# A two-layer graph kernel on one core: layer 0's sum as seven half-block products instead of sixty-four tile products

## The chip, the cores and the metric

The kernel runs on one core of a Trainium2 chip. The metric is the device time of one execution in microseconds (us); before the change it is 1270.91 us, the median of three runs (1270.83 to 1271.21). The core has a matrix engine (TensorE, PE in the profile; PEld is its weight load), two engines for elementwise work on which much depends here (VectorE, DVE; ScalarE, ACT), GpSimd (POOL) and a queue engine (SyncE, SP) that issues most transfers. Each engine takes its instructions in order and waits for the others by semaphores.

## What is computed

There are 16 batches; each has 1024 nodes with 256 features (`x`) and an integer adjacency matrix `adj` (1024 x 1024, symmetric, ones on the diagonal, otherwise 0 or 1). Two layers follow one another, each with a residual sum and a normalization of the row:

```
# layer 0
e     = leaky(einsum('bid,bjd->bij', h * a[:, 0], h))     # a = a0 where adj == 1
alpha = sigmoid(where(adj == 1, e, -big))
x     = layernorm(x + einsum('bij,bjd->bid', alpha, h) + bias)
# layer 1
Hh    = einsum('bni,io->bno', x, W)
s, d  = Hh . a_src, Hh . a_dst
e     = where(adj != 0, exp(-leaky_relu(s[:, :, None] + d[:, None, :])), 0)
x     = layernorm(x + elu(einsum('bnm,bmo->bno', e, Hh) / rowsum(e)))
```

All products are in f32. A second path in the file covers adjacency values of 2 to 4 and doesn't run for these inputs.

## The kernel before, in words

Rows of 128 nodes are tiles: NT = 8 tiles a batch, HT = 4 tiles in a half; the features are ND = 2 pieces of 128. The order of the instructions is written out by hand, with no scheduler. Batch `b` runs layer 0 beside layer 1 of the batch before (`prev`) and the last normalization of the one before that (`done`). One turn of the loop over `b` has three stages on PE.

- **Strips.** `strip(b, jt)` makes row tile `jt` of the logits, from its diagonal to the right (L233: transposed x against x scaled by a0). ACT makes two tanh of it (L241, L242), VectorE takes their maximum (L243), and `finish` adds one, multiplies by the adjacency and writes `al` (L249). That is twice the sigmoid; the part below the diagonal is the mirror image of the part above it: `dump` transposes it in 32 x 32 squares on VectorE (L265) and sends it to DRAM in four transfers (L269), `gather` reads it back into `al` (L273), one strip later in the SP queue, and `mask` multiplies it by its adjacency (L280). Between the strips stand the eight `project` of layer 1 for `prev` (L411), and `share_p`, which sends a row of 1024 numbers to all partitions through DRAM (L431, L433).
- **Layer 0's sum.** `sum0` for each of the eight row tiles: `multiply0` is eight products of 128 x 128 by 128 x 256 into one accumulator (L348), `end0` halves it, adds the bias on VectorE (L358) and takes mean and variance (L301, L303). Two identities on the diagonal of `al`, added by GpSimd (L259), bring in the residual x. GpSimd takes the roots of the variances (L310 to L327), ACT scales the rows (`scale0`, L331). The rows go to DRAM (`save_x1`, L376) and come back in blocks of 32 (`fetch_x1`, L120), which VectorE turns (`turn_x1`, L387) into the transposed form that `project` needs. `weights` (L460, eight a batch, on VectorE) makes layer 1's matrix `e` meanwhile, `check_adj` runs on ACT.
- **Layer 1's sum.** For each of the eight row tiles eight products of 128 x 128 by 128 x 257 (L465). `elu` inverts the row sum on VectorE (L488, L489) and evicts the tile twice on ACT (L497, L498); `add` finishes the row and its statistics on VectorE (L503, L505, L301, L303).

`x` has two buffers (`load_x`, L94), so the next batch's x is loaded while this one is summed. `al`, `xT`, `xa`, `x1T` have one each. PSUM: three banks for strips (`ps_e`), two for `ps_t`, three for accumulators (`ps_acc`).

Of the kernel before, what the change touches and what calls it, by code (L numbers as in the profile page):

```python
# [18 lines left out]
P = 128  # L19
# [11 lines left out]
def one_kind_pass(  # L31
# [57 lines left out]
    def load_x(b, queues):  # L89
        xs[b] = two.tile([P, NT, D], F32, tag="x", name=f"x_{b}")  # L90
        rows = x[b].rearrange("(t p) d -> p t d", p=P)
        n = NT // len(queues)
        for g, queue in enumerate(queues):
            queue.dma_start(xs[b][:, ts(g, n), :], rows[:, ts(g, n), :])  # L94
# [43 lines left out]
    arow = two.tile([P, D], F32, tag="h", name="arow")[0:ND, 0:P]  # L138
    nc.scalar.dma_start(arow, a0.rearrange("(c p) o -> c (p o)", p=P))
# [16 lines left out]
    nc.vector.memset(ones, 1.0)  # L156

    warm = const.tile([P, 1], F32, tag="warm", name="warm")
# [4 lines left out]
    load_x(1, [nc.gpsimd])  # L163
# [4 lines left out]
    pcol = ps_e.tile([P, HALF], F32, tag="e", name="pcol")[:, 0:ND]  # L168
    nc.tensor.transpose(pcol, arow, ident[0:ND, 0:ND])
    nc.scalar.copy(acol, pcol)  # L170
# [11 lines left out]


# [9 lines left out]
    def turn_x(b, c):  # L193

        if c == 0:
            xas[b] = one.tile([P, ND, N], F32, tag="xa", name=f"xa_{b}")
        nc.vector.transpose(xTs[b][:, c, :], xTs[b][:, c, :])
        nc.scalar.mul(xas[b][:, c, :], xTs[b][:, c, :], acol[:, c : c + 1])
# [46 lines left out]
    def finish(b, jt, c0=0, c1=N):  # L245


        c0 = max(c0, jt * P)
        nc.vector.scalar_tensor_tensor(  # L249
            als[b][:, jt, c0:c1],  # L250
            tbs[b, jt][:, c0 - jt * P : c1 - jt * P],
            1.0,
            adjs[b, jt // HT][:, jt % HT, c0:c1],
            ALU.add,
            ALU.mult,
        )
        if c0 == jt * P:
            diag = als[b][:, jt, ts(jt, P)]
            nc.gpsimd.tensor_tensor(diag, ident2, diag, ALU.add)  # L259
# [17 lines left out]
    def mask(b, t):  # L277
        for js, rows in adj_rows(b, t + 1, NT, ts(t, P)):
# [27 lines left out]
    def rstd(mv, what):  # L306
# [3 lines left out]
        nc.gpsimd.tensor_scalar(ve, mv[:, :, 1], EPS, None, ALU.add)  # L310
# [10 lines left out]
    def center(mv, what):  # L321

        r = rstd(mv, what)
# [3 lines left out]
        nc.gpsimd.tensor_scalar(mr, mr, -1.0, None, ALU.mult)  # L327
        return [(r[:, t : t + 1], mr[:, t : t + 1]) for t in range(n)]
# [4 lines left out]
    x1s, mv0s, r0s = {}, {}, {}  # L333
# [3 lines left out]
    def sum0(b, t):  # L337
        multiply0(b, t)
        end0(b, t)

    def multiply0(b, t):
        if t == 0:
            x1s[b] = two.tile([P, NT, D], F32, tag="x1", name=f"x1_{b}")
            mv0s[b] = small.tile([P, NT, 2], F32, tag="mv0", name=f"mv0_{b}")
            r0s[b] = []
# [10 lines left out]
    def end0(b, t):  # L356
        y = x1s[b][:, t, :]
        nc.vector.scalar_tensor_tensor(y, accs[t], 0.5, bias_bc, ALU.mult, ALU.add)  # L358
        stats(y, mv0s[b][:, t, :], f"0_{b}_{t}")
        if t % HT == HT - 1:  # L360
            g = t // HT
            r0s[b] += center(mv0s[b][:, ts(g, HT), :], f"0_{b}_{g}")
# [3 lines left out]


    x1Ts, Hs, pqs, p_bcs, es = {}, {}, {}, {}, {}

    x1_rows = {}  # L370
# [26 lines left out]
    def project(b, t):  # L397
# [11 lines left out]
        pt = ps_acc.tile([P, D + 2], F32, tag="acc", name=f"pH_{b}_{t}")  # L409
# [9 lines left out]
        nc.scalar.activation(w, pt[:, 1:2], AF.Exp, scale=-SLOPE)  # L419
        nc.scalar.activation(pqs[b][:, :, t], pt[:, 0:2], AF.Exp, scale=SLOPE - 1.0)  # L420
        nc.scalar.mul(Hs[b][t][:, 0:D], pt[:, 2:], w)
# [51 lines left out]
    def elu(b, t, acc):  # L473

        if t == 0:
# [8 lines left out]
            mv1s[b] = small.tile([P, NT, 2], F32, tag="mv1", name=f"mv1_{b}")  # L484


        rinv = small.tile([P, 1], F32, tag="rinv", name=f"rinv_{b}_{t}")
        nc.vector.tensor_scalar(rinv, acc[:, D : D + 1], TINY, None, ALU.max)  # L488
        nc.vector.reciprocal(rinv, rinv)  # L489
# [40 lines left out]
    nc.sync.dma_start(bias_bc, bias.partition_broadcast(P))  # L530

# [12 lines left out]
    for t in range(NT):  # L544
# [12 lines left out]
        if t < 2:  # L557
            make_Wx(t)
        if t == 1:
# [4 lines left out]
        if t in (4, 5):  # L564
            scale0(0, 2 * t - 8)
            scale0(0, 2 * t - 7)
            turn_x(1, t - 4)
        if t == 5:
            save_x1(0, 0)
            fetch_x1(0, 0)  # L570

    for b in range(1, B):
# [3 lines left out]
        projects = [[0, 1], [2], [3], [4, 5], [6], [7], [], []]  # L576
        if prev == 0:

            projects = [[], [], [0, 1], [2, 3], [4, 5], [6, 7], [], []]
        for jt in range(NT):  # L580
            if jt == 4:
                mask(b, 0)
            strip(b, jt)
            if prev == 0 and jt < 2:
                scale0(0, HT + 2 * jt)
                scale0(0, HT + 2 * jt + 1)
            finish(b, jt)
# [4 lines left out]
            if prev == 0 and jt == 2:  # L592
                transpose_x1(0)
            if jt >= 1:
                gather(b, jt - 1)
            for t in projects[jt]:
                project(prev, t)
            if jt == 6:
                share_p(prev)
            if jt >= 6:  # L600
                mask(b, jt - 5)
        check_pq(prev)
        if not last:
            load_x(b + 1, [nc.sync])
# [3 lines left out]
        for t in range(NT):  # L608
            if 1 <= t < 5:
                mask(b, t + 2)  # L610
            for m in ([], [], [0, 1], [2], [3], [4], [5], [6, 7])[t]:
                weights(prev, m)
            if done >= 0:
                scale1(done, t)
                if t in (3, 7):
                    store(done, t - 3, HT)
            sum0(b, t)
            if t == 5 and not last:
                load_adj(b + 1, 0)
            if t in (5, 6):  # L620
                scale0(b, 2 * t - 10)
                scale0(b, 2 * t - 9)
            if t == 6:
                save_x1(b, 0)
            if t >= NT - CHECKS:
                check_adj(b, t - NT + CHECKS)
        if not last:
            load_adj(b + 1, 1)


        for t in range(NT):
            acc = acc1(prev, t, ps_acc, "acc")
            for m in range(NT):
                sum1(prev, t, acc, m)
            if last and t == 6:
                turn_x1(b, 1)
            if last and t == 3:
                turn_x1(b, 0)
            if last and t == 7:
                for m in range(2):  # L640
                    weights(b, m, 0, HT)
            elu(prev, t, acc)
            if last and t == 7:
                for m in range(2, 6):
                    weights(b, m, 0, HT)
            if t >= 1:
                add(prev, t - 1)
            if t == 0:
                fetch_x1(b, 0)
            if t in (1, 2):  # L650
                scale0(b, 2 * t + 2)
                scale0(b, 2 * t + 3)
            if t == 2:
                save_x1(b, 1)
            if t == 4:
                fetch_x1(b, 1)
                if not last:
                    turn_x1(b, 0)
            if not last and t in (3, 5):
                turn_x(b + 1, (t - 3) // 2)  # L660
            if not last and t == 6:
                turn_x1(b, 1)
            if last and t in (4, 6):
                t0 = (t - 4) // 2 * HT
                for n in range(HT):
                    project(b, t0 + n)
                share_half(b, t0)
        if not last:
            add(prev, NT - 1)
            r1s[prev] = center(mv1s[prev], f"1_{prev}")  # L670
# [520 lines left out]
```

## Time and profile before

| what | value |
|---|---|
| median of three runs | 1270.91 us |
| span of the profiled execution | 1268.6 us |
| one turn of the loop over b (600.37 to 678.40 us) | 78.03 us |
| of it: strips and projections | 22.56 us |
| of it: layer 0's sum | 27.63 us |
| of it: layer 1's sum | 27.84 us |
| VectorE busy in the turn | 58.20 us |
| ScalarE busy in the turn | 40.56 us |
| GpSimd busy in the turn | 17.89 us |

The loop makes fifteen such turns, from about 54 us to 1225 us; batch 0's layer 0 stands before them and batch 15's layer 1 behind them. An f32 product of 128 x 128 by 128 x n appears as two records in the profile, so the 64 products of a sum are 128 records.

### The profile page before, as it was taken

What the parts mean: (1) busy time and instruction counts of PE and PEld (TensorE: products, weight loads), DVE (VectorE), ACT (ScalarE), POOL (GpSimd) and SP (SyncE); (2) the same over time, 40 slices, a digit from 0 to 9 for tenths busy, and PEclk for the clock granted to TensorE, in tenths of its full rate; (3) what the DMA queues carried; (4) which work ended last, traced back from release to release, by engine and by line L of the source; (5) the groups of instructions that cost most, each with busy time, mean ns of one, the idle gap of its engine ahead of it and who ended that gap; (6) DMA issues with size and microseconds to landing.
All of it is one profiled execution on the core that took longest, in us unless ns stands there. A gap on an engine that the chain in (4) does not pass through costs nothing.

```text
span 1268.6 us, 17528 instructions
## 1 busy us (share of the span) xinstructions
PE 1259.2 (99%) x5476; PEld 1024.5 (81%) x5476; DVE 925.2 (73%) x2027; ACT 650.2 (51%) x1467; POOL 299.7 (24%) x605
## 2 busy tenths in 40 slices
PE   9999999999999999999999999999999999999997
PEld 7788787887878878788787887878778787887886
DVE  5686867868678686876868868687686877858657
ACT  4645645456353564545645445454455644456434
POOL 2212231212312122121222212223122231212213
PEclk9999999999999999999999999999999999999999
DMA  9489595795959869497694966949579595895422
GB/s 213 80 171 155 92 197 92 168 185 106 190 90 177 168 124 198 78 174 159 131 203 83 184 131 139 210 80 190 113 167 185 97 192 95 171 183 99 109 51 69
DMA packets 603832, 180.77 MB, mean 142 GB/s; under 512 B 482010, under 2 KB 585940, under 8 KB 603732
## 3 DMA queue, kind: packets, MB, share of 16 engines
q1 hardware_dynamic: 581760, 135.85, 54.4%
q0 software_dynamic: 21280, 43.06, 18.7%
q8 instruction: 46, 0.75, 0.3%
q10 hardware_dynamic: 692, 0.66, 0.1%
q14 instruction: 54, 0.44, 0.1%
HBM read 152.44 MB, written 60.62 MB: 168 GB/s over the span
## 4 chain that ended last, share of the span: by engine, by line
PE 98%; DVE 1%; ACT 0%; issue 0%; ACTq 0%; DVEq 0%
PE acc L348 35%; PE acc L465 34%; PE pe L233 20%; PE pH L411 9%; PE busy L146 0%; PE pal L288 0%; PE pxT L209 0%; DVE st L301 0%; DVE y L505 0%; DVE y L503 0%; PE prow L427 0%; ACT y L331 0%; ACT y_kept L331 0%; ACT L680 0%; DVE mv L303 0%
## 5 line engine op out<-in xcount | busy, mean ns | idle before, releaser
L348 PE MATMUL acc<-x,al 128*128 128x256 f32 x2048 | 445.5, 379 | 0.0
L465 PE MATMUL acc<-H,e 128*128 128x257 f32 x2032 | 444.9, 379 | 0.0
L465 PEld LDWEIGHTS acc<-H,e 128*128 128x128 f32 x2032 | 384.9, 189 | 56.9
L348 PEld LDWEIGHTS acc<-x,al 128*128 128x128 f32 x2048 | 387.5, 190 | 51.8
L233 PE MATMUL pe<-xa,xT 128*128 128x384 f32 (+1 forms) x720 | 251.0, 486 | 0.0
L233 PEld LDWEIGHTS pe<-xa,xT 128*128 128x128 f32 x720 | 132.7, 189 | 80.9 <-issue 42.6
L331 ACT ACTIVATE x<-x,mr,r 128x256 f32<-128x256 f32 x128 | 69.4, 592 | 227.2 <-POOL mr L327 227.2
L460 DVE SCALAR_TENSOR_TENSOR e<-p,pq_kept,adj 128x1024 f32<-128x1024 f32 (+1 forms) x136 | 160.8, 1208 | 25.4 <-DMA p<-p_row 25.4
L310 POOL TENSOR_SCALAR ve<-mv 128x4 f32<-128x4 f32 (+2 forms) x49 | 16.2, 332 | 622.8 <-DVE mv L303 616.2
L497 ACT ACTIVATE h<-acc,rinv 128x256 f32<-128x256 f32 x126 | 59.1, 469 | 200.5 <-DVE rinv L489 185.1
L241 ACT ACTIVATE tb<-pe 128x512 f32<-128x512 f32 (+1 forms) x192 | 94.1, 490 | 120.3 <-PE pe L233 91.1
L488 DVE TENSOR_SCALAR rinv<-acc 128x1 f32<-128x1 f32 x127 | 19.9, 157 | 157.3 <-PE acc L465 156.8
L243 DVE TENSOR_TENSOR tb<-tb,low 128x512 f32<-128x512 f32 (+1 forms) x192 | 103.4, 544 | 38.6 <-ACT low L242 38.3
L128 ACT ACTIVATE junk<-adj,minus 128x2048 bf16<-128x2048 bf16 x64 | 127.3, 1989 | 0.0
L411 PE MATMUL pH<-Wx,x1T 128*128 128x258 f32 x512 | 126.3, 381 | 0.0
L411 PEld LDWEIGHTS pH<-Wx,x1T 128*128 128x128 f32 x512 | 97.2, 190 | 35.8 <-issue 14.3
L259 POOL TENSOR_TENSOR al<-ident,al 128x128 f32<-128x128 f32 x128 | 66.6, 520 | 227.2 <-DVE al L249 226.7
L249 DVE SCALAR_TENSOR_TENSOR al<-tb,adj 128x512 f32<-128x512 f32 (+7 forms) x132 | 97.5, 739 | 5.3 <-DVE tb L243 0.4
L242 ACT ACTIVATE low<-pe 128x512 f32<-128x512 f32 (+1 forms) x192 | 93.2, 485 | 0.5 <-DVE tb L243 0.5
L280 DVE SCALAR_TENSOR_TENSOR al<-al,adj 128x512 f32<-128x512 f32 (+3 forms) x150 | 76.1, 531 | 21.8 <-DMA al<-mir 21.7
L358 DVE SCALAR_TENSOR_TENSOR x<-acc,bias_bc 128x256 f32<-128x256 f32 x128 | 53.9, 421 | 41.5 <-PE acc L348 41.0
L265 DVE STREAM_TRANSPOSE tb<-tb 128x896 f32<-128x896 f32 (+6 forms) x105 | 74.7, 712 | 3.6
(110 smaller groups left out, 954.0 us busy)
## 6 DMA issues: line engine op xcount, KB each, us to landing
adj<-in_adjT POOLq DMA_DIRECT2D x30, 1024.0 KB, 10.3
x_rows<-x SPq DMA_DIRECT2D x31, 512.0 KB, 3.7
x1T<-x_rows SPq DMA_DIRECT2D x248, 64.0 KB, 2.6
out<-y_kept SPq DMA_DIRECT2D x30, 512.0 KB, 6.4
x<-in_x SPq DMA_DIRECT2D x14, 1024.0 KB, 6.0
xT<-in_x SPq DMA_DIRECT2D x112, 128.0 KB, 4.9
p<-p_row POOLq DMA_DIRECT2D x15, 512.0 KB, 4.5
mir<-tb SPq DMA_DIRECT2D x60, 112.0 KB, 3.0
```

What stands on the lines that cost most here:

```text
L128: nc.scalar.activation(junk, rows, AF.Square, bias=minus1, scale=2.0, accum_out=chk[:, b * CHECKS + n : b * CHECKS + n + 1],)
L233: nc.tensor.matmul(pe[:, 0:w], lhsT=xTs[b][:, c, ts(jt, P)], rhs=xas[b][:, c, ds(jt * P + o, w)], start=(c == 0), stop=(c == ND - 1),)
L241: nc.scalar.activation(tb[:, ds(o, w)], pe[:, 0:w], AF.Tanh, scale=0.5)
L242: nc.scalar.activation(low[:, 0:w], pe[:, 0:w], AF.Tanh, scale=0.5 * SLOPE)
L243: nc.vector.tensor_tensor(tb[:, ds(o, w)], tb[:, ds(o, w)], low[:, 0:w], ALU.max)
L249: nc.vector.scalar_tensor_tensor(als[b][:, jt, c0:c1], tbs[b, jt][:, c0 - jt * P : c1 - jt * P], 1.0, adjs[b, jt // HT][:, jt % HT, c0:c1] ...
L265: nc.vector.transpose(tb, tb)
L280: nc.vector.scalar_tensor_tensor(v, v, 1.0, rows, ALU.add, ALU.mult)
L348: nc.tensor.matmul(acc, lhsT=als[b][:, jt, ts(t, P)], rhs=xs[b][:, jt, :], start=(jt == 0), stop=(jt == NT - 1),)
L411: nc.tensor.matmul(pt, lhsT=x1Ts[b][:, c, ts(t, P)], rhs=Wx[:, c, :], start=(c == 0), stop=(c == ND - 1),)
L460: nc.vector.scalar_tensor_tensor(e, p_bcs[b][:, cols], q, rows, ALU.mult, ALU.min)
L465: nc.tensor.matmul(acc, lhsT=es[b][:, m, ts(t, P)], rhs=Hs[b][m], start=(m == 0), stop=(m == NT - 1),)
```

## The change

Layer 0's sum is regrouped. With `al` and x cut in halves, the product of 2 x 2 blocks is made from seven block products instead of eight, with sums of blocks before and after. The result stands transposed (features on the partitions, nodes along the row), which is the form that `project` needs; the rows are what is now fetched through DRAM. The core of the diff:

```diff
-        xs[b] = two.tile([P, NT, D], F32, tag="x", name=f"x_{b}")
+        xs[b] = one.tile([P, NT, D], F32, tag="x", name=f"x_{b}")
...
+    def combine_x(b, n):
...
+        nc.vector.tensor_tensor(out_, in0, in1, op)
+    def combine_al(b, k, j0, j1):
...
+        out_, in0, in1 = {1: (t1, t1, m12), 2: (t1, m21, t1), 3: (m12, t1, m12), 4: (m21, m22, t1)}[k]
+        nc.vector.tensor_tensor(out_, in0, in1, ALU.subtract)
+    def product(b, k):
...
+        for jt in range(HT):
+            nc.tensor.matmul(
+                banks[bank],
+                lhsT=lhs[:, jt, :],
+                rhs=rhs[:, jt, :],
...
+    def unite(b, what):
...
+    def turn_y(b, g, queue=nc.sync):
...
+        nc.vector.transpose(Zs[b][:, :, half], yTs[b][:, :, half])
...
+                queue.dma_start(
+                    v[c, q], Zs[b][ts(q, SQ), c, half].rearrange("p (nb e) -> p nb e", e=SQ)
+                )
...
-        projects = [[0, 1], [2], [3], [4, 5], [6], [7], [], []]
+        projects = [[0, 1], [2], [3], [4, 5], [6, 7], [], [], []]
...
             if jt == 4:
-                mask(b, 0)
+                mask(b, 0, 0, HT)
+                combine_al(b, 1, 0, 2)
+            if jt == 5:
+                new_yT(b)
+                product(b, 1)
+                share_p(prev)
+                mask(b, 1, 0, HT)
+                mask(b, 2, 0, HT)
+                combine_al(b, 1, 2, HT)
+                for t in range(3):
+                    mask(b, t, HT)
...
+            if jt == 6:
+                unite(b, "p1")
+                product(b, 5)
+                unite(b, "p5")
+                mask(b, 3, HT)
+                combine_al(b, 2, 0, HT)
             strip(b, jt)
...
+        product(b, 3)
+        combine_al(b, 3, 0, HT)
+        extras(0)
+        product(b, 6)
+        weights(prev, 0)
+        mask(b, 4)
+        mask(b, 5)
+        combine_al(b, 4, 0, 2)
+        weights(prev, 1)
+        mask(b, 6)
+        combine_al(b, 4, 2, HT)
+        unite(b, "u2")
+        extras(1)
+        product(b, 7)
+        extras(2)
+        product(b, 2)
+        extras(3)
+        unite(b, "s")
+        unite(b, "c12")
+        unite(b, "c22")
+        unite(b, "c11")
+        product(b, 4)
+        turn_y(b, 0)
+        if not last:
+            load_x(b + 1, [nc.sync])
+        weights(prev, 2)
+        weights(prev, 3)
...
+        weights(prev, 4)
+        unite(b, "c21")
+        turn_y(b, 1)
+        fetch_y(b, 0)
+        fetch_y(b, 1)
+        check_adj(b, 3)
+        weights(prev, 5)
...
+            combine_x(b + 1, 3)
+        first = [acc1(prev, t, *((ps_acc, "acc") if t in (1, 2) else (ps_t, "t"))) for t in range(HT)]
+        for m in range(NT):
+            for t in range(HT):
+                sum1(prev, t, first[t], m)
```

`combine_x` makes four block sums of x, 128 x 512 each; `combine_al` those of `al`; `product` is four products of 128 x 128 by 128 x 512; `unite` takes the seven products together, "p1", "p5" and "c11" on ACT, "u2", "s", "c12", "c22" and "c21" on VectorE, 128 x 512 each. `extras(n)` holds the scalings of `prev` and `done` and `check_adj`, all on ACT. Product 4 adds to the bank that product 7 wrote, and "s" reads that bank between the two. Because the result is not scaled before `project`, the mean is taken out of W once, before the loop (`center_Wx`), and the row's factor enters layer 1's exponentials and H (`rcols`, eight more one-column ACT instructions a batch); `end0`'s halving goes into four times the epsilon. The first four row tiles of layer 1's sum run together, step by step over `m`; their four row sums are copied by ACT and inverted by one VectorE instruction. The statistics of layer 0's rows move into layer 1's sum (`stats0`), and the masks are split between the halves of `al`. Batch 0 keeps the old form of the sum.

## The prediction

> **What bounds the kernel now.** I read the page first: the engines' totals, the clock by slices, and the chain that ended last.
>
> ```profile
> PE 1259.2 (99%) x5476; PEld 1024.5 (81%) x5476; DVE 925.2 (73%) x2027; ACT 650.2 (51%) x1467; POOL 299.7 (24%) x605
> ...
> PEclk9999999999999999999999999999999999999999
> ...
> PE 98%; DVE 1%; ACT 0%; issue 0%; ACTq 0%; DVEq 0%
> ```
>
> PE is never idle, at full clock, and the chain is PE alone: time comes off only where PE has less to do, and any new wait of PE counts in full. VectorE has room, but only 27% of the span. So I cut one turn of the loop into its three stages:
>
> ```profile
> core 0: us, PE busy (x) PEld busy (x) DVE busy (x) ACT busy (x) POOL busy (x), PEclk, DMA share, GB/s
> 600.37:622.93 22.56, 22.56 (x82) 14.85 (x81) 18.97 (x34) 15.75 (x48) 6.89 (x13) 1.00 0.56 101
> 622.93:650.56 27.63, 27.63 (x130) 24.33 (x129) 22.77 (x47) 12.42 (x23) 7.68 (x14) 1.00 0.97 185
> 650.56:678.40 27.84, 27.84 (x129) 24.25 (x128) 16.46 (x46) 12.39 (x23) 3.31 (x9) 1.00 0.77 152
> ```
>
> In order: strips and projections, layer 0's sum, layer 1's sum; 78.03 us together, VectorE 58.20 of them. DMA is full in the second stage. Prices come from the groups kept apart by shape:
>
> ```profile
> L348 PE MATMUL acc<-x,al 128*128 128x256 f32 x2048 | 445.5, 379 | 0.0
> L460 DVE SCALAR_TENSOR_TENSOR e<-p,pq_kept,adj 128x1024 f32<-128x1024 f32 x120 | 149.9, 1270 | 25.4 <-DMA p<-p_row 25.4
> L358 DVE SCALAR_TENSOR_TENSOR x<-acc,bias_bc 128x256 f32<-128x256 f32 x128 | 53.9, 421 | 41.5 <-PE acc L348 41.0
> L243 DVE TENSOR_TENSOR tb<-tb,low 128x512 f32<-128x512 f32 x64 | 43.7, 683 | 21.6 <-ACT low L242 21.6
> L243 DVE TENSOR_TENSOR tb<-tb,low 128x384 f32<-128x384 f32 x80 | 42.7, 535 | 13.2 <-ACT low L242 13.2
> L249 DVE SCALAR_TENSOR_TENSOR al<-tb,adj 128x1024 f32<-128x1024 f32 x15 | 18.4, 1226 | 1.7 <-DVE tb L243 0.4
> ```
>
> The reader is to see the idle column too: VectorE waits here for PE and ACT, never the reverse.
>
> **What the change takes from PE.** The timeline of PE shows eight records of 512 columns (strip 0, 600.37 to 603.80) in 3.43 us: the size of one block product. Seven are 24.03 instead of 27.63 us: 3.60 off a turn, 54.0 in fifteen. Centering W adds two products of 258 columns (0.87, as one projection: 612.00 to 612.87 in PE's timeline) once. With no wait the turn would be 74.43 us.
>
> **What it puts on VectorE.** The largest f32 tensor_tensor in the trace is 128x512 (683 ns). From 512 to 1024 columns L249 grows by 536 ns (690 to 1226, the first from its 512 group), so 1024 is 1.22 and 2048 is 2.29; the other bound for 2048 is two of 1226, 2.45. I take the first. A turn gains four sums of al of 1024 and two of 2048 (9.46), four of x of 512 (2.73) and five unions of 512 (3.43): 15.62. It loses eight L358 (3.37), four row-sum clips of 157 ns and three reciprocals of 164 (1.12): 4.49. Net 11.1: VectorE goes from 58.20 to 69.3 in a turn of 74.4. It still fits, so what counts is where PE must wait for it.
>
> **Off the path.** ACT gains three evictions of 512 (0.60 each) and twelve columns (0.17): 3.8, to 44.4 of 74. GpSimd gains six small products (0.2): 1.2. Both end far below the turn; uncovered they would cost those sums. SP issues as many transfers as before (sixteen writes of blocks and two reads of rows, for two writes and sixteen reads), with the same bytes. The four joined row tiles cost PE nothing (same products); the fewer weight loads neither, since PEld is hidden today.
>
> **Where PE would wait.** I count us from the turn's first strip product (600.37). PE alone would reach product 1 at 19.85 (strip 4 ends at 18.11, two projections of 0.87), product 5 at 24.67, product 3 at 29.40, product 7 at 36.26, product 2 at 39.69, product 4 at 43.12; layer 1's sum would end at 74.39. Product 4 may start only after VectorE's "s", and VectorE takes its queue in order. That queue hangs on the gathers:
>
> ```profile
> 619.15 1.16 DVE L280 SCALAR_TENSOR_TENSOR al<-al,adj 128x384 f32<-128x384 f32 x2 [1.21 <-DMA al<-mir]
> ...
> 681.78 0.66 DVE L243 TENSOR_TENSOR tb<-tb,low 128x512 f32<-128x512 f32 x1
> ```
>
> ```profile
> 614.66 0.42 SPq L273 DMA_DIRECT2D al<-mir  x1
> 615.56 3.09 SPq L269 DMA_DIRECT2D mir<-tb  x4
> 618.76 0.44 SPq L273 DMA_DIRECT2D al<-mir  x1
> 619.25 2.36 SPq L269 DMA_DIRECT2D mir<-tb  x4
> 621.72 0.53 SPq L273 DMA_DIRECT2D al<-mir  x1
> ```
>
> VectorE, in the first fence, stands idle for the first gather, 18.8 into the turn. The third gather is issued at 21.35 behind the writes of strip 3 and takes 3.7 (median of that size): 25.05. Now `mask(b, 2, 0, HT)` waits for it, ahead of everything else. From there to the end of "s" VectorE has, in its new order: mask 0.27, half sum 1.22, three masks 2.06, strip 5 1.54, mask 0.69, sum 2.29, strips 6 and 7 1.73, sum 2.29, weights 1.25, two masks 1.02, half sum 1.22, weights 1.25, mask 0.27, half sum 1.22, two unions 1.37: 19.7. Means overlap a little: all instructions of the old turn add up to 60.9 and were busy 58.2, a factor of 0.956, so 18.8, and "s" ends at 43.9. Two more waits lie there: the sixth gather, issued behind strip 6's writes, lands at about the time its mask comes up (0 to 1), and each handover costs about 0.1; 0.9 in all, so 44.8. PE stands 1.7 us in front of product 4. The earlier points are passed with little room: product 5's second half wants its sum at 26.4 and gets it at 26.5, product 3 its mask at 29.4 and gets it at 30 to 30.8, product 7 its sum at 36.3 and gets it at 36.5. These waits are not added, since PE's wait at the last point contains them.
>
> **The reload of x** is the second place. x has one buffer now, so the load can't start before product 4 ends (48.2), and in SP's queue it stands behind eight writes of turn_y (47.5; eight transfers of that size took 4.62 us at 668.05): issued at 52.1, landed 5.6 to 6.0 later, 58. VectorE comes to `combine_x` at 57.3 (44.8, plus 1.37 + 1.24 + 2.4 + 0.5 + 1.25 + 0.69 + 1.24 + 3.8) and waits 0.8. What is queued behind it: the turning of x, the reciprocal for the four joined tiles, the statistics, all of `add`, and through them the next strips. Worked on (combine_x 2.73, turn 2.46, statistics 2.2 twice, four inversions 0.28 and eight `add` at 1.45), VectorE ends at 80.7, 4.6 us after the turn of 76.1; today it is 3.4 (681.78 in the fence above, PE having begun the strips at 678.40). The difference dies out, since VectorE idles 1.4 us for ACT in strips 0 and 1 today (0.70, 0.30, 0.38). Today the load lies in its second buffer and is late for nothing.
>
> **A rule against it.** The first 14 records of 128 columns took 3.36 us, 0.24 each, where 16 transposes of the same width after them took 2.52 us, 0.16 each: PE starts slowly, and only there. By the Trainium skill, "TensorE: Matmul & The Clock Gate", Part 1, PE falls back to half clock after an idle window of about 3.4 us and needs another to recover. Waits under 2 us would not bring that about; were it reached once a turn, my estimate from that page is 1.7 us a turn, 26 us in all. No row of this trace shows a fallback, because PE is never idle in it.
>
> **The sum.** 1268.6 - 15 x (3.60 - 1.7) = 1240.1; plus 0.9 for W; plus 2 for the edges, where batch 1's x is loaded only after batch 0's sum and the last batch does all statistics before its first inversion (0 to 4 by the 6.0 of a load against strip 0's 3.4 head start). That is 1243.0 in the span. The median lies 2.3 above the profiled span. 1245.3.
>
> **Rivals.** *No wait at all* (chance 0.16): the gathers land a microsecond earlier because strips reach VectorE sooner, and overlap on VectorE is better than 0.956. 1268.6 - 54.0 + 0.9 + 2.3 = 1218, up to 1228. For it: each point is missed by under 2 us. Against: an idle VectorE at 18.8 is measured. *My forecast* (0.50), waits of 1 to 2.6 a turn: 1229 to 1262. *Even* (0.11): waits of 3 to 3.7, if the gathers come 1.5 later, as the 3.70 us for four writes at 622.30 in SP's list shows they can: 1262 to 1275. *The reload of x becomes the bound* (0.23): DMA ran at 0.97 to full in the old second stage, and now x, both adjacency halves and sixteen block writes fall together. `x<-in_x` took 16.5 us in its one other issue. With x 5 us later than I have it, VectorE's 69.3 plus some 10 of waits (5.8 x, 1.2 and 1.0 gathers, 2 rows fetched late) makes a turn of 79.5, since VectorE's queue then closes the loop from batch to batch: 1268.6 + 15 x 1.5 + 0.9 + 2 + 2.3 = 1296. It decides from 3.6 us of PE wait a turn, which is x some 3 us later than in my sum; I give it 1275 to 1300. That the change does not do what it says is excluded for PE: the order of the built program has 28 products of 512 columns in place of 64 of 256.
>
> **How the numbers follow.** I predict 1245; the forecast's own range is 1229 to 1262. The range is 1221 to 1280, reaching into the cases on both sides. About 0.2% (2.5 us) is what can be told from no change. Faster: 0.16 + 0.50 + 0.06 = 0.72; same 0.05; slower 0.23.
>
> **What would show it.** Layer 0's seven products 24.0 us a turn; VectorE busy 68 to 71 in a turn; PE idle 1 to 2.6 a turn, before product 4, released by VectorE's "s"; sums of 2048 at 2.2 to 2.5 us. I am wrong if PE's idle time is before the strips or released by x or the fetched rows (the reload), or if a clock below full shows in the slices.

## The result: 8% slower, and the profile after

| what | before | after |
|---|---|---|
| median | 1271.06 us | 1374.49 us (1370.18 to 1375.34) |
| span of the profiled execution | 1268.6 us | 1372.1 us |
| one turn, mean of fourteen between the starts of layer 1's sums | 78.04 us | 85.34 us |

The ratio is 1.0806, with a 95% interval of 1.079 to 1.0821. The forecast was 1245. What happened is nearest to the rival "the reload of x becomes the bound": VectorE's queue closes the loop from turn to turn. It cost more than the 1275 to 1300 given for it, and x alone is not what held the queue, as the experiments show.

The page of the changed kernel, in the order in which the page before was read:

```profile
PE 1251.0 (91%) x4400; PEld 820.2 (60%) x4400; DVE 1067.0 (78%) x2030; ACT 719.9 (52%) x1701; POOL 359.8 (26%) x702
...
PEclk9999999999999999999999999999999999999999
...
DVE 45%; SPq 19%; DMA 13%; PE 8%; ACT 7%; issue 5%; POOL 2%; DVEq 0%; ACTq 0%; POOLq 0%
```

PE is idle 121.1 us (1372.1 less 1251.0; before: 9.4), and the chain that ended last, PE alone before, now runs through VectorE, SP's queue and transfers. Who waited for what, in all (us, times, longest):

```profile
DVE S L421 <- DMA x<-in_x: 135.1, 14, 12.5
ACT h L667 <- DVE sums L649: 124.0, 15, 10.9
...
DVE al L303 <- DMA al<-mir: 55.3, 30, 3.0
...
DVE st L324 <- DMA x<-y_rows: 38.0, 15, 6.1
...
PE pV L451 <- DVE al L429: 34.7, 14, 3.1
...
PE pe L252 <- ACT xa L217: 27.3, 14, 4.8
...
PE pe L252 <- ACT y_kept L668: 21.6, 14, 1.8
```

VectorE waits 9.7 us a turn for x, 4.0 for the gathers, 2.7 for the fetched rows; PE waits for ACT, which waits for VectorE (124.0 us in front of the joined reciprocals alone). One turn in four stretches (columns as before: each engine's busy time, granted clock, DMA share):

```profile
645.81:672.50 26.69, 24.86 (x75) 14.74 (x76) 24.06 (x57) 19.95 (x59) 5.86 (x19) 0.94 0.40 71
672.50:700.29 27.79, 24.50 (x64) 11.27 (x64) 24.16 (x34) 18.67 (x33) 11.69 (x14) 1.00 0.79 147
700.29:715.00 14.71, 14.71 (x69) 12.90 (x68) 8.33 (x11) 2.04 (x6) 1.62 (x2) 1.00 1.11 225
715.00:731.25 16.25, 13.25 (x61) 11.19 (x60) 10.19 (x25) 4.01 (x9) 2.73 (x8) 1.00 0.66 140
```

In the third stretch the transfers are full (share 1.11) and VectorE works 8.3 of 14.7 us; in the first they are at 0.40, and the clock is below full. SP's queue there (start, time in issue):

```profile
699.25 5.72 SPq L499 DMA_DIRECT2D y_rows<-Z  x8
705.07 2.72 SPq L94 DMA_DIRECT2D x<-in_x  x1
707.89 13.76 SPq L499 DMA_DIRECT2D y_rows<-Z  x8
721.70 2.15 SPq L507 DMA_DIRECT2D x<-y_rows  x2
```

x was issued at 705.07, and VectorE's next instructions show when it and the rows were there:

```profile
717.53 0.69 DVE L421 TENSOR_TENSOR S<-x 128x512 f32<-128x512 f32 x1 [8.73 <-DMA x<-in_x]
...
725.61 0.43 DVE L324 BATCH_NORM_STATS2 st<-x 128x6 f32<-128x256 f32 x1 [3.12 <-DMA x<-y_rows]
```

x took 12.4 us from issue to use; GpSimd issued the two adjacency halves at 701.84 and 709.10, in the same stretch. Behind these two stand the adds of layer 1 and with them PE's next strips:

```profile
666.29 1.88 PE L252 MATMUL pe<-xa,xT 128*128 128x512 f32 x4
...
679.03 1.98 PE L451 MATMUL pV<-al,S 128*128 128x512 f32 x4 [2.56 <-DVE al L429]
680.85 1.47 PE L252 MATMUL pe<-xa,xT 128*128 128x256 f32 x8
683.05 3.67 PE L451 MATMUL pV<-al,S 128*128 128x512 f32 x8 [0.72 <-ACT low L261]
...
693.42 3.60 PE L451 MATMUL pQ<-al,x 128*128 128x512 f32 x8
696.85 3.60 PE L451 MATMUL pW<-al,x 128*128 128x512 f32 x8
700.29 27.96 PE L622 MATMUL acc<-H,e 128*128 128x257 f32 x128
731.58 3.47 PE L252 MATMUL pe<-xa,xT 128*128 128x512 f32 x4 [3.33 <-ACT xa L217]
```

The last line shows a second loss: four records that take 1.88 us at full speed (666.29) took 3.47 after 3.33 us of idleness. PE's granted clock was 0.62 from 731.58 to 733.00 and 0.50 from there to 735.10.

### The profile page after: what moved, and what is told of

Its sections match the earlier page's. It is cut to its first block, busy times and chain, and to the rows that moved or that the text cites. A ratio compares the mean times of both kernels' runs of the same rounds, so it can differ in the third digit from the quotient of the medians.

```text
span 1372.1 us, 15671 instructions
## 1 busy us (share of the span) xinstructions
PE 1251.0 (91%) x4400; PEld 820.2 (60%) x4400; DVE 1067.0 (78%) x2030; ACT 719.9 (52%) x1701; POOL 359.8 (26%) x702
## 4 chain that ended last, share of the span: by engine, by line
DVE 45%; SPq 19%; DMA 13%; PE 8%; ACT 7%; issue 5%; POOL 2%; DVEq 0%; ACTq 0%; POOLq 0%
SPq L499 16%; DVE e L617 7%; DVE st L324 6%; DVE al L268 5%; DVE tb L262 5%; DMA al<-mir 4%; DMA x<-y_rows 4%; DVE al L429 4%; DVE tb L288 3%; DMA mir<-tb 3%; DVE y_kept L675 3%; DVE al L303 3%; PE acc L622 3%; DVE mv L326 3%; SPq L292 3%
## 5 line engine op out<-in xcount | busy, mean ns | idle before, releaser
L252 PE MATMUL pe<-xa,xT 128*128 128x384 f32 (+1 forms) x720 | 270.9, 512 | 48.9 <-ACT xa L217 27.3
L282 POOL TENSOR_TENSOR al<-ident,al 128x128 f32<-128x128 f32 x128 | 90.5, 711 | 315.5 <-DVE al L268 220.6
L451 PE MATMUL pV<-al,S 128*128 128x512 f32 x240 | 122.5, 647 | 39.8 <-DVE al L429 34.7
L429 DVE TENSOR_TENSOR al<-al 128x1024 f32<-128x1024 f32 (+1 forms) x90 | 141.9, 1577 | 7.1 <-DVE al L303 0.5
L556 PE MATMUL pH<-Wx,yT 128*128 128x258 f32 x480 | 119.9, 384 | 8.2 <-ACT y_kept L668 8.2
L667 ACT ACTIVATE h<-acc,sums 128x256 f32<-128x256 f32 x60 | 28.5, 475 | 178.6 <-DVE sums L649 124.0
L556 PEld LDWEIGHTS pH<-Wx,yT 128*128 128x128 f32 x480 | 90.9, 192 | 45.2 <-issue 15.1
L451 PE MATMUL pW<-al,x 128*128 128x512 f32 x240 | 108.4, 594 | 0.0
L451 PE MATMUL pQ<-al,x 128*128 128x512 f32 x240 | 107.9, 592 | 0.0
L451 PEld LDWEIGHTS pV<-al,S 128*128 128x128 f32 x240 | 46.0, 202 | 96.2 <-DVE al L429 46.3
```

The costliest lines, as they stand in the source:

```text
L252: nc.tensor.matmul(pe[:, 0:w], lhsT=xTs[b][:, c, ts(jt, P)], rhs=xas[b][:, c, ds(jt * P + o, w)], start=(c == 0), stop=(c == ND - 1),)
L429: nc.vector.tensor_tensor(out_, in0, in1, ALU.subtract)
L451: nc.tensor.matmul(banks[bank], lhsT=lhs[:, jt, :], rhs=rhs[:, jt, :], start=first and jt == 0, stop=jt == HT - 1, skip_group_check=True,)
L556: nc.tensor.matmul(pt, lhsT=x1Ts[b][:, c, ts(t, P)], rhs=Wx[:, c, :], start=(c == 0), stop=(c == ND - 1),)
```

## The experiments

Each is the changed kernel with the edit shown. A single time is that of one execution, with executions of the kernel before beside it (medians 1270.94 to 1271.57); a ratio is to the kernel before, with its 95% interval. Executions of one kernel lie up to 12 us apart (e12: 1295.47 to 1307.55), so two single times that differ by 10 us do not rank their kernels.

**Is it the queue, the place of the sums, or the traffic?**

```diff
 e2_x_act
-            load_x(b + 1, [nc.sync])
+            load_x(b + 1, [nc.scalar])
```

> The reload of x is issued on ScalarE's own queue at the same place, so it no longer stands behind the eight writes of turn_y: issued at the end of product 4 (700.3 in the turn read, instead of 705.1). Theory A (the single buffer puts x in VectorE's way, and the queue order is half of it): x lands up to 4.8 us earlier, VectorE's wait for x falls from 9.6 us a turn to 5 to 7, time falls from 1374 by 14 x 3 to 5, to 1305 to 1335. Rival B (DMA is simply full there and x takes what is left): the load lasts as much longer as it starts earlier, wait and time stay within 1 us a turn, 1360 to 1380.

1385.42 us. VectorE's wait for x is gone, and its wait for the rows rose from 38.0 to 160.4. Neither expectation: the wait moved, and the time did not fall. In one turn x was used 8.2 us after its issue (704.19 to 712.42) without a wait. But SP's sixteen block writes alone now kept its queue until 22.6 us after their start (702.96 to 725.51), as long as the writes and the load did together before (699.25 to 721.70: 22.5). The Trainium skill, "DMA: Bandwidth & Descriptors", section "Issuing engines are not separate DMA queues", says that another issuing engine saves issue time and no transfer time; this run agrees.

```diff
 e3_no_adj
+        if b >= 4:
+            adjs[b, g] = adjs[b - 2, g]
+            return
```

> Leaves out the adjacency loads of batches 4 to 15, which take the adjacency of the batch two before; the output changes, no instruction on the compute engines does. Theory A: x still waits for product 4 and for the queue; its 12.4 us fall to 5.6 or 6, as before the change, and the wait of 9.6 a turn falls to 3 or 4; 1374 falls by 12 x 6 to about 1300. Rival B (the block writes of the rows, not the adjacency, are what x shares the engines with): x still takes 10 to 12 us, time over 1350.

1270.87 us, less than the 1300 of theory A. The adjacency of batches 4 and up is left out (older batches' serve instead). Transfers of this kernel, median us to landing, and then those of the changed kernel:

```profile
x<-in_x SPq DMA_DIRECT2D x15, 1024.0 KB, 5.9
y_rows<-Z SPq DMA_DIRECT2D x240, 64.0 KB, 2.5
```

```profile
x<-in_x SPq DMA_DIRECT2D x15, 1024.0 KB, 12.3
y_rows<-Z SPq DMA_DIRECT2D x240, 64.0 KB, 4.2
```

Without the adjacency, x lands in the 5.9 us that the prediction had put in, and 104 us go. The block writes of the rows, too, land in 2.5 us in place of 4.2. So the late landing, of x and of the rows, is made by what is transferred beside them.

```diff
 e4_sums_in_strips
-            if jt < 4 and b == 1:
+            if jt < 4:
                 combine_x(b, jt)
...
-            combine_x(b + 1, 0)
```

(all four sums of the next x leave layer 1's sum)

> The four block sums of x stand in the first four strips of their own batch, as batch 1 has them, instead of ahead of the turning of x; the load itself is not moved. Theory A says that VectorE stands in its queue behind x: its wait for x goes to 0. But the fetched rows of layer 0 are issued behind x in SP's queue (721.7) and land at 725.6, and their statistics come next: if A's second half holds, that wait grows from 3 to about 10 us and only 1 to 3 us a turn are won, 1330 to 1360. Rival C (the rows are late only because VectorE itself is late): the rows' wait stays at 3 and 9 us a turn are won, 1245 to 1260.

1384.31 us. The wait for x is gone, that for the rows is 160.1: VectorE no longer stands in front of x, and stands in front of the rows instead. Theory A's second half is seen in the wait; its 1330 to 1360 missed, since nothing was won.

```diff
 e5_x_last (e4 and:)
-        if not last:
-            load_x(b + 1, [nc.sync])
...
         fetch_y(b, 1)
+        if not last:
+            load_x(b + 1, [nc.sync])
```

> As the run before, and the load of x is issued behind the two fetches of the rows in SP's queue. Theory A (both waits of VectorE in layer 1's sum come from the order x, rows): x is needed only in the next strips, the rows land near 713 to 716, both waits go below 2 us a turn, the turn falls from 85.4 to 75 to 78, time 1235 to 1270. Rival B (DMA is full and the rows wait for bandwidth): rows' wait 5 us or more, time over 1300. Rival C (VectorE has too much work for the turn): PE still waits 6 us or more a turn with VectorE never idle, over 1310.

1349.41 us, ratio 1.0619 (1.0599 to 1.0638): rival B's range. With x behind everything else, 25 us came back, and the rows still hold VectorE for 118.6 us.

**One buffer, the traffic, or the order of VectorE's queue?**

```diff
 e6_two_x (and three buffers of tb, half the scratch of check_adj)
-        xs[b] = one.tile([P, NT, D], F32, tag="x", name=f"x_{b}")
+        xs[b] = two.tile([P, NT, D], F32, tag="x", name=f"x_{b}")
...
+            load_x(b + 1, [nc.sync])
             new_xT(b + 1)
...
-        if not last:
-            load_x(b + 1, [nc.sync])
```

> The changed kernel with two buffers of x again, the load back at its old place in front of the transposed blocks (before layer 0's sum); the room comes from three buffers of tb, the row of W's means in another buffer, and the adjacency's range test in eight pieces with half the scratch. Theory A (one buffer of x forces 1 MB into the stretch that also holds two adjacency halves and the rows, and VectorE stands in front of it): VectorE's 135 us of waiting for x goes, the landing of the rows falls below 4 us, and the turn loses most of its 9 us of waiting: 1255 to 1290. Rival B (whatever is moved, the rows written and fetched in this stretch come late by themselves, so the wait only changes its name, as it did with x on another queue): the wait for fetched rows rises above 120 us in all and the time stays at 1340 or above.

1396.64 us. x now lands in 5.8 us and nothing waits for it, and yet, among the waits of e6:

```profile
DVE st L325 <- DMA x<-y_rows: 174.6, 16, 13.5
...
PE pe L253 <- ACT xa L218: 63.3, 14, 6.1
```

Theory A had named the single buffer; that part of it fell. The rows alone hold the queue as long as x and the rows did together, as rival B said. Since the range test in eight pieces also gives ACT more work (742.1 us busy for 719.9), the 22 us above the changed kernel are not all the rows'.

```diff
 e7_adj_late (e5 and:)
+            if jt == 0 and b > 1:
+                load_adj(b, 1)
...
-            load_adj(b + 1, 1)
```

> The order of e5_x_last, and the second adjacency half of the next batch is loaded only in its own strip 0 (it is first needed in strip 4), so layer 1's sum has one adjacency half in place of two. Theory A (the DMA engines are full in layer 1's sum, and what lands last sets VectorE's queue): the landing of the fetched rows falls from 4.9 to about 3 us, VectorE's wait for them from 118.6 us to 30 to 60, time 1275 to 1305. Rival B (the rows are late by the chain write, fetch, statistics, however free the engines are): the wait stays over 100 us and the time within 15 us of 1349.

VectorE's wait for the rows in e7 (us in all, times, longest):

```profile
DVE st L324 <- DMA x<-y_rows: 50.6, 16, 5.8
```

1279.67 us, 70 below e5: with one adjacency half less in layer 1's sum the block writes land in 3.2 us (e5: 4.9), and the wait falls as theory A said.

```diff
 e8_rows_late (e5 and:)
-            for t in range(HT):
-                stats0(b, t)
-            roots0(b, 0)
         for t in range(NT):
...
+            if t == 5 and not last:
+                for q in range(HT):
+                    stats0(b, q)
+                roots0(b, 0)
```

(and the statistics of tiles 4 to 7 behind the last `add`, the projections one strip later)

> The order of e5_x_last, all loads unchanged, but the statistics of the fetched rows stand later in VectorE's queue: those of tiles 0 to 3 behind the sixth row tile of layer 1, those of 4 to 7 at the end, and the projections that want their roots come one strip later. Theory C (the queue's order is what costs: the rows are late for the place where they are asked for, not for their use): the 118.6 us wait for rows goes to under 15, and the time falls to 1245 to 1285 with the transfers as slow as before. Theory A alone (bandwidth; the wait goes on to the next thing loaded, x or the adjacency of the next strips): waits for x or for the mask's and gather's transfers of over 60 us take its place, and the time stays over 1300.

1272.26 us, 77 below e5, with the writes as slow as there (5.0). VectorE's wait for rows is 5.6 in all. Theory C holds: late rows cost because VectorE was told to look at them before its other work. e7 took off nearly as much in the old order by making them less late, so late rows and this order cost only together.

> e7 and e8 together: x loaded last, the second adjacency half in the next strips, the statistics of the rows late in VectorE's queue. If bandwidth and order share the cost, this beats each alone and comes to 1230 to 1265, a turn of 75 to 77 us, near the 74.4 of PE's work, with the clock at 0.99 or above. If something else bounds the loop (VectorE's own 67 to 69 us of work with its short waits, or the wait of PE before product 5's second half), it stays at 1270 or above with PE idle at that place.

e9_both (e7 and e8 together): 1343.8 us, ratio 1.0575 (1.0558 to 1.0593). Two cures that each gave some 70 us or more nearly cancelled. What follows is read from the two traces; no run tested it. In e9 GpSimd comes to the load of the second half late, since the roots of tiles 4 to 7 stand before it: at 639.59, 12 us into the strips (e7: 604.61, 3 us in). There it meets the mirrored blocks. SP's queue, the first eight of their writes in e9, and in e7:

```profile
636.82 11.21 SPq L292 DMA_DIRECT2D mir<-tb  x8
```

```profile
612.47 5.89 SPq L292 DMA_DIRECT2D mir<-tb  x8
```

VectorE's wait for the gathers is 96.0 us (e7: 31.3), PE's before product 5 is 82.2 (34.4).

**What holds e8 at 1272?** PE waits mainly before product 5 (30.5 us), VectorE waits 53.0 us in front of the joined reciprocals, and it begins the strips late.

```diff
 e10_three_joined (e8 and: three tiles, not four, summed together)
-            for t in range(HT):
+            for t in range(3):
                 sum1(prev, t, first[t], m)
```

> e8_rows_late with three row tiles of layer 1 summed together in place of four. In e8 VectorE stands 53.0 us (14 times, up to 4.3) in front of the reciprocals of the joined tiles and has 19 us of work behind them, while PE waits only before product 5. Theory D (VectorE's queue closes the loop and the join holds it up): with three tiles the sums are read 3.4 us earlier, the 53.0 us fall to under 15, the gathers come earlier in PE's terms, PE's wait before product 5 (30.5) falls by half or more, and the time goes to 1230 to 1255. Rival E (the gathers' transfers set product 5 wherever VectorE stands): the wait before product 5 stays near 30 us and the time within 8 us of 1272. If the third tile catches up with the weights, PE waits in layer 1's sum by up to 1 us a turn.

1282.38 us: theory D missed (1230 to 1255). The 53.0 us went, and 40.5 of waiting for PE's later tiles and 46.4 for ACT's evictions came (e8: 39.4 of the latter).

```diff
 e11_gather_early (e8 and: half of strip 2's writes on GpSimd, gather(b, 2) before dump(b, 3))
+            queue = nc.gpsimd if t == 2 and a % 2 else nc.sync
...
+            if jt == 3:
+                gather(b, 2)
```

> e8_rows_late with four tiles joined as before; the four writes of strip 2's transposed block are shared between SP's and GpSimd's queues, and the third gather is issued in front of strip 3's writes. Rival E: VectorE's wait for gathers (31.4 us) and PE's wait before product 5 (30.5) fall together by 15 us or more, time 1245 to 1260. Theory D: the wait before product 5 may shrink, but VectorE, late from the turn before, closes the loop elsewhere, with PE waiting at the strips: 1262 to 1272.

1292.09 us. SP now stands in front of the gather until the writes have landed, and the writes of strips 3 and 4 stand behind it:

```profile
628.17 5.30 SPq L297 DMA_DIRECT2D al<-mir  x2
633.52 4.44 SPq L293 DMA_DIRECT2D mir<-tb  x8
```

PE's wait before product 5 fell from 30.5 to 19.4, and waits before product 3 took its place.

> Both: three joined tiles and the earlier third gather, on e8's order. If the two effects add, PE's waits fall below 15 us in all and the time to 1222 to 1245, near the 74.4 us a turn that PE's own work allows and below the kernel before. If they are the same microseconds, it equals the better of the two.

Both together: 1299.67 us, ratio 1.0234 (1.0191 to 1.0277). As far as single times tell, the effects add (10 and 20 us above e8), in the wrong direction.

```diff
 e13_three_fill (e10 and: rows' statistics where VectorE idles)
-            if t == 5 and not last:
-                for q in range(HT):
-                    stats0(b, q)
-                roots0(b, 0)
+            if t in (5, 6) and not last:
+                for q in range(HT):
+                    stats0(b, (t - 5) * HT + q)
+                roots0(b, t - 5)
             if t >= 1:
                 add(prev, t - 1)
```

> e10_three_joined, with the statistics of the fetched rows moved into the places where VectorE idles in layer 1's sum: tiles 0 to 3 in front of the fifth add, 4 to 7 in front of the sixth, in place of behind the fifth and behind the last. In e10 VectorE idles 0.9, 1.7 and 2.1 us there for PE and ACT, and begins the strips 6.3 us behind PE (in the kernel before: 3.4). Theory D (VectorE's queue closes the loop; with three joined tiles its idle time was only moved, not used): the statistics fill the idle time, VectorE begins the strips 2 to 4 us behind PE, PE's wait before product 5 falls from 34.6 us to under 15, time 1235 to 1262. Rival E (the gather's own transfers set product 5): the wait stays above 25 us and the time at 1270 to 1285. If the rows are not there yet, the wait for them is back (over 30 us in all) and it is no faster than e10's 1282.

1270.64 us, ratio 0.9992 (0.9983 to 1.0001): 12 below e10, even with the kernel before, short of the 1262 expected. PE's wait before product 5 is 22.6.

```diff
 e14_fill_pool (e13 and:)
-        nc.vector.tensor_tensor(out_, in0, in1, op)
+        (nc.gpsimd if b > 1 else nc.vector).tensor_tensor(out_, in0, in1, op)
```

> e13_three_fill with the four sums of x on GpSimd from batch 2 on, which takes 2.7 us a turn off VectorE and puts four sums of 128x512 on GpSimd, whose price no run here shows: its 128x128 products take 0.71, so 1.5 to 2.9 each. Theory D: VectorE gains up to 2.6 us a turn, and the time goes 5 to 35 us below e13's, as far as product 5 still waits for VectorE. If GpSimd's sums are slow or stand in front of its diagonal products, PE waits for S before product 5 or for al, and the time is the same as or above e13's.

1281.2 us, ratio 1.0083 (1.0057 to 1.011). GpSimd's sums took 1.27 to 1.69 us (VectorE: 0.65), at the lower bound and below it, and VectorE was busy longer, 1085.5 us (1073.5), though it had 56 instructions less. Three of its groups by shape in e14, and in e13:

```profile
L262 DVE TENSOR_TENSOR tb<-tb,low 128x384 f32<-128x384 f32 x80 | 63.8, 812 | 3.3 <-ACT low L261 3.3
L262 DVE TENSOR_TENSOR tb<-tb,low 128x512 f32<-128x512 f32 x64 | 53.2, 848 | 8.1 <-ACT low L261 8.1
...
L268 DVE SCALAR_TENSOR_TENSOR al<-tb,adj 128x1024 f32<-128x1024 f32 x15 | 29.8, 1987 | 0.6
```

```profile
L262 DVE TENSOR_TENSOR tb<-tb,low 128x384 f32<-128x384 f32 x80 | 42.7, 550 | 3.5 <-ACT low L261 3.5
L262 DVE TENSOR_TENSOR tb<-tb,low 128x512 f32<-128x512 f32 x64 | 42.3, 678 | 7.9 <-ACT low L261 7.9
...
L268 DVE SCALAR_TENSOR_TENSOR al<-tb,adj 128x1024 f32<-128x1024 f32 x15 | 18.4, 1224 | 0.6
```

These run beside GpSimd's sums and are 25 to 62% longer; others kept their times.

```diff
 e15_late_adds (e13 and: the adds of tiles 6 and 7 in the next turn)
                 mask(b, 1, 0, HT)
+                if done >= 0:
+                    add(done, NT - 2)
+                    add(done, NT - 1)
                 mask(b, 2, 0, HT)
```

> e13_three_fill, with the last two adds of layer 1 (2.9 us of VectorE) moved out of the tail, where the next strips stand behind them, into the next turn in front of the mask that waits 3.0 us for the third gather. Theory D' (the loop closes from PE's last tile over VectorE's tail, the strips, their dumps and the third gather back to PE's product 5; in e13 that is 673.5 to 701.9 us, 28.4, behind 49.1 of PE without a wait): VectorE begins the strips about 2.9 us earlier, so does the gather, and PE's wait before product 5 (22.6) nearly goes: 1228 to 1252, faster than the kernel before. Rival E (the gather's transfers or VectorE's total): the wait before product 5 stays above 15 us, 1262 or above.

1267.33 us, ratio 0.9976 (0.9966 to 0.9985): with e16 the only versions that beat both kernels, by a quarter of a per cent.

VectorE's and PE's waits in e15:

```profile
DVE tb L262 <- ACT low L261: 46.2, 40, 2.2
...
PE pV L451 <- DVE al L429: 23.2, 14, 2.9
...
PE pV L451 <- ACT low L261: 10.1, 14, 0.7
...
DVE al L303 <- DMA al<-mir: 5.6, 8, 2.3
```

Half of theory D' held: VectorE waits for the strips now, no longer for gathers (e13: 37.2). The other half did not: PE's wait is as long as in e13, and it is rival E's wait (above 15 us) and time (1262 or above) that came. Behind the adds VectorE comes to the third gather's mask at about the time when it lands.

> The same with four joined tiles, as in the change: VectorE idles up to 4.3 us in front of the joined reciprocals and nothing fills it. If the join costs, this is 8 to 25 us above e15; if the late adds free the loop whatever the join does, the two are within 5 us.

The same with four joined tiles: 1267.49 us, ratio 0.9975 (0.9966 to 0.9985). The join of the change costs nothing here.

```diff
 e17_hole (e15 and: only the add of tile 7 late)
-            if jt < 4:
-                combine_x(b, jt)
+            if jt == 0:
+                combine_x(b, 0)
...
+                for n in range(1, 4):
+                    combine_x(b, n)
                 mask(b, 2, 0, HT)
```

> e15_late_adds with only the last add left for the next turn (the one before goes back into the tail, where VectorE now waits 2.0 us for the first strip), and three of the four sums of x moved from strips 1 to 3 to the place in front of the mask that waits for the third gather. In e15 VectorE no longer waits for the gathers (5.6 us in all), it is busy from strip 0 to the sum that product 5 waits for, 23.3 us on end, and PE still waits 23.2 us there. Theory F (what sets product 5 is the amount of VectorE's work between strip 0 and that sum; strip 2's block is turned and dumped behind it): 1.4 us less of it, and strip 2's dump 1.3 us earlier, takes PE's wait there to under 8 us: 1235 to 1258. Rival G (the third gather, 9.6 us from turned block to landing, sets it, whatever VectorE does in front): the wait for gathers comes back to 20 us or more in all, PE's wait stays above 15 us, 1260 to 1270.

> The same with four joined tiles, as in the change. e15 and e16 were equal within 1 us, so theory F and rival G both expect this within 5 us of e17_hole; if VectorE's idle time before the joined reciprocals (51.4 us) is what is left, e17 is the faster by 5 to 15.

e17: 1273.53 us, ratio 1.0012 (1.0 to 1.0025); e18, with four joined tiles: 1270.48 us, 0.9996 (0.9985 to 1.0008). In e17 the wait for gathers is back at 24.7 us and PE's before product 5 is 26.0, as rival G said, with a time 3.5 us above G's range; theory F (under 8 us of wait, 1235 to 1258) fell. e18 shows 25.3 and 26.6. Together with e13 and e15 this leaves one reading, argued and not shown: whether VectorE waits for the third gather or works in front of it, PE gets its sum at about the same time. What sets that time within the gather's chain (write, landing, read) was not taken apart further, so a cure for it stays open.

## Why the prediction was wrong

- **PE's saving** was right. Products start 3.43 us apart (693.42, 696.85, 700.29 above), 24.0 for seven. Yet PE's busy time fell by only 8.2 us. e15 issues the same 4400 products and is busy 1216.6, 34.4 less (the strip products of 512 columns average 656 ns in the changed kernel and 592 in e15). Most of this is the lower clock, some 24 us by the last point here; the rest, in it products that start behind a wait (1.98 for 1.88 above), was not taken apart.
- **VectorE's new work** was priced right. The large sums of the changed kernel, in the groups kept apart by shape (put in: 1.22 and 2.29 us):

```profile
L429 DVE TENSOR_TENSOR al<-al 128x1024 f32<-128x1024 f32 x60 | 73.3, 1222 | 5.5 <-DVE al L303 0.5
L429 DVE TENSOR_TENSOR al<-al 128x2048 f32<-128x2048 f32 x30 | 68.6, 2286 | 1.6
```

  VectorE was busy 66.75 of a turn (put in: 69.3).
- **The wait before product 4** is absent: product 4 follows product 2 at 696.85 with no gap. PE's wait is two points earlier, in front of product 5's second half (2.56), which the prediction had listed as passed by 0.1 us. That point is nearer to the third gather, and the gather came 31.5 us after the strips' start (677.35, the mask behind it), not 25.05: VectorE enters the strips 11.0 us behind PE (put in: 4.6), so everything it dumps is late:

```profile
656.78 1.26 DVE L262 TENSOR_TENSOR tb<-tb,low 128x512 f32<-128x512 f32 x2
```

- **The step that failed** is the transfers in layer 1's sum, in two terms. The first, the reload of x, was mis-sized: "issued at 52.1, landed 5.6 to 6.0 later, 58. VectorE comes to `combine_x` at 57.3 ... and waits 0.8." Measured after the strips' start: issued at 59.3, VectorE there at 63.0, x used at 71.7. That is a landing of 12.4 and a wait of 8.7 in this turn, 9.7 on average. Of the 7.9 us more, 6.4 are the landing and 1.5 the issue, which came 7.2 later where VectorE came 5.7 later. The landing was taken from loads with no adjacency beside them (in the kernel before x is issued at 634.07, the adjacency halves at 644.17 and 655.00). e3 shows the cause: without the adjacency the same load takes 5.9.

  The second term, the wait for the rows that come back through DRAM, stood at nothing in the forecast, without a reason; only the rival gave it 2 us. This term set the time. By the prediction's own terms the statistics of the rows begin 15.4 us after product 4 (58.1 + 2.73 + 2.46 + 0.28 less 48.2). The means of fourteen turns, from the start of layer 1's sum to VectorE's first use of the rows:

| kernel | rows used after, us | time, us |
|---|---|---|
| changed | 25.1 | 1374.49 |
| e2, e4, e6 (no wait for x) | 25.6, 25.5, 26.5 | 1385.42, 1384.31, 1396.64 |
| e5 (x behind the rows) | 22.6 | 1349.41 |
| e7 (and one adjacency half less) | 17.7 | 1279.67 |
| e3 (no adjacency; mean of twelve turns without it) | 16.3 | 1270.87 |

  Taking away the wait for x alone won nothing, for the rows came no earlier. Nor was the forecast reached where the rows' lateness was gone (e3) or harmless (e8): both took 1271 to 1272 us, and PE's largest wait there, 13.0 and 30.5 us, is the one before product 5. The kernel before showed two prices for eight transfers of the rows' size, and the prediction took the lower. The higher one stands beside the adjacency half issued at 655.00; in the changed kernel the second eight took 13.76 us (707.89):

```profile
656.27 8.38 SPq L120 DMA_DIRECT2D x1T<-x_rows  x8
...
668.05 4.62 SPq L120 DMA_DIRECT2D x1T<-x_rows  x8
```

- **Behind it, the end of VectorE's turn.** "The difference dies out" failed too: what stands behind x and the rows (the adds, by way of ACT the next strips) is the next turn's start, so the delay is handed on. The reading "VectorE waits here for PE and ACT, never the reverse" is right for PE and overlooks ACT, which stood in front of VectorE's reciprocals before the change already, at no cost to PE then. By this way the delay reached PE:

```profile
ACT h L497 <- DVE rinv L489: 185.1, 89, 3.3
```

  e8 showed that the order of VectorE's queue has its part: 77 us went with the transfers as slow as before. Two of the signs that the prediction had named for being wrong came: PE idle before the strips, and a clock below full (0.94 in the first stretch).
- **The rival's price.** It had named the mechanism and worked out a turn of 79.5 (its terms, 69.3 and 10.0, add up to 79.3) with 10 us of waits on VectorE: 5.8 for x, 2.2 for gathers, 2 for rows. Measured: 9.7, 4.0 and 2.7, 16.4 together, which with the rest of the sum unchanged makes 85.9 where 85.3 was measured. So close a match is partly luck: VectorE's own work was 2.5 less than put in, and some 2 us of other waits took its place. The reason, "x has one buffer now", was not the cause: e6 gave x its second buffer and its old place, and was no faster. The rows' way through DRAM now ends where they are asked for at once, with the joined tiles' adds behind; before, VectorE came to `turn_x1` when the blocks were there, and waited 1.4 us for them in all.
- **The clock rule** mattered. The Trainium skill, "TensorE: Matmul & The Clock Gate", Part 1, states half clock after an idle window of about 3.4 us. The trace agrees at 731.58 (3.33 us idle, double time, granted clock 0.50), and a wait of 2.56 left the speed alone (1.98 at 679.03). The prediction's "Waits under 2 us would not bring that about" did not hold at 649.80 (last section). Its estimate of 26 us in all stood outside the sum; the granted clock, 0.981 over 1372.1 us here and 0.998 over 1266.3 in e15, makes it some 24, an estimate.

## What to carry to other kernels

Price a moved transfer by what will be in flight beside it, and ask of every in-order queue what stands behind the instruction that waits for it. Three cures took away the wait for x (another queue, a later use of x, a second buffer) and gave nothing, since the rows behind it came no earlier. With x loaded last, asking for the rows later gave 77 us, and moving one large load out of the full stretch gave 70. Two cures are not a sum: tried together they gave 6. When the removed work is 3.6 us a turn out of 78, the extra dependencies have to cost less than that; the best version found kept 0.4 (e15: 77.65 a turn for 78.04).

## What the runs showed of the hardware

- GpSimd working on f32 sums of 128 x 512 slowed VectorE's instructions with two inputs beside it, 678 to 848 ns and 1224 to 1987 ns (means of groups, e13 to e14). The Trainium skill, "GPSIMD Engine Reference", Specifications, says that the two share SBUF interfaces, with contention when VectorE's instruction has two SBUF inputs; these rows agree.
- The clock can fall to half after short waits as well: in the changed kernel four strip records took 3.61 us at 649.80, with the granted clock at 0.56 from there to 651.60 and 0.50 to 653.40. In front of them stood waits of 1.01 and 1.83 us only, with another of 2.37 us shortly before.
